# The output projection of two attentions in seven block products instead of eight

## The chip, the core and the metric

The kernel runs on one core of a Trainium2 chip, as one launch. The metric is the device time of that launch in microseconds. All data is float32. The engines are called by the profile's names: PE (TensorE matmuls), PEld (TensorE weight loads), DVE (VectorE), ACT (ScalarE), POOL (GpSimd) and SP (SyncE, which issues most of the DMAs).

## The reference

Four transformer layers run one after the other over x of shape (4, 256, 256) with a context of the same shape. The first layer, which the change touches, has two cross attentions and an MLP:

```python
B, D, H, K = 4, 256, 16, 128            # 4 batches of 256 tokens, 256 features, 16 heads of 128

def _cross_attention(q_in, kv_in, wq, bq, wk, bk, wv, bv, wo, bo, bias_k, bias_v):
    qh = (q_in @ wq + bq).reshape(b, q_len, H, K)      # wq, wk, wv: 256 x 2048
    kh = (kv_in @ wk + bk).reshape(b, t, H, K)
    vh = (kv_in @ wv + bv).reshape(b, t, H, K)
    kh = jnp.concatenate([kh, jnp.broadcast_to(bias_k, (b, 1, H, K))], axis=1)   # one learned key
    vh = jnp.concatenate([vh, jnp.broadcast_to(bias_v, (b, 1, H, K))], axis=1)   # and value
    logits = jnp.einsum('bqhk,bthk->bhqt', qh, kh) / sqrt(K)
    weights = jax.nn.softmax(logits, axis=-1)
    ctx = jnp.einsum('bhqt,bthk->bqhk', weights, vh).reshape(b, q_len, H * K)
    return ctx @ wo + bo                               # wo: 2048 x 256

x = x + _cross_attention(layer_norm(x), ctx, ...)      # first attention
x = x + _cross_attention(layer_norm(x), ctx, ...)      # second attention
x = x + gelu(layer_norm(x) @ w_fc1 + b_fc1) @ w_fc2 + b_fc2
...                                                    # three more layers, heads of 16 and 8 features
```

`ctx @ wo` is what the change computes in another way.

## The kernel before

**Tasks and a planner.** The kernel is written as a list of `Task` objects. A task has PE work (`run`, with a shape and an estimated length in us), the tasks it comes after, buffers that it takes from rings and gives back, and `Post` steps: work of another engine on what PE has left in PSUM, with estimated lengths in ns, such as an add on DVE. A Post may name two engines; the planner then takes the one that ends it first. `plan` goes through the tasks with a model of each engine's clock and writes down one order. Each engine then runs its own instructions strictly in that order (`Pinned` keeps them in program order). The table `HANDICAPS` steers the order: a number for each batch in each stage, one for each kind of task, and four general ones: `near` (a reserve, in us, that is added before a task counts as ready), `slack`, `solo` (a penalty for running one half of a pair of narrow products alone) and `wide` (a factor on the Posts' lengths). Nearly all instructions are issued through `Pinned`, so that the profile gives them all the same line, L134; tiles tell them apart.

**The first two attentions.** The loop over `li` runs over the two attentions, that over `hg` over four groups of four heads, and that over `bp` over two pairs of batches. For each group the weights are loaded into one of two sets of tiles (`W0`: `wv`, `wq`, `wk`, `wo` and others), by DMAs of SP. For each pair of batches V, q and k are each made by `seven`: two matrices are cut into 2 x 2 blocks, and the product of blocks is made in seven block products instead of eight, with sums of blocks made before on POOL (`sums`, `value_sums`) or on DVE or POOL (`differences`, `context_sums`), and sums of the products on DVE and ACT.

Then, for each batch and each half of its queries (128 rows), four heads are scored on PE (128 x 257, the learned key included), DVE takes the maximum of each row, ACT the exponential, and `quotients` on DVE multiplies each row by the reciprocal of its sum. The scores of one half lie in one tile `E` of the ring `E0`. For each head, the four 128 x 128 blocks of `E` of both halves are then transposed on PE (`turns`), copied to `eT`, and multiplied with V (`weighted`). The result of a head, 128 features x 256 tokens, is put into `cT` (ring `CT`) with its bias added.

**The projection.** When all four heads of a batch are in `cT`, `project` (task of 3.46 us) multiplies it with the group's `wo`: for each of two tiles of 128 tokens, four matmuls, one for each head, with 128 tokens as the stationary operand and 256 features as the moving one, all summed in PSUM. That fills one PSUM bank of 128 x 512. `add` on DVE then adds the bank to `X`, the residual, in one instruction. The projections come 2 x 4 x 4 = 32 times.

PSUM has eight banks, handed out by the ring `PS`. Of the buffers: `E0` has four tiles, `XN` (for the layer norm's output) three, `CT` two, and each of the two sets of weights has its own `bvl`, the row of learned values that is subtracted from the bias row `bvb`.

After the two attentions come the layer's MLP and the other three layers, planned in the same way, in stages 1 to 6 of the table.

Of the kernel before, what the change touches and what calls it, by code (L numbers as in the profile page):

```python
# [11 lines left out]
ALU = mybir.AluOpType  # L12
# [3 lines left out]
P = 128  # L16
B, S, D = 4, 256, 256
# [34 lines left out]
def kernel(ctx: ExitStack, tc: tile.TileContext, a: dict, out: bass.AP):  # L52
# [85 lines left out]
    def pe(out, lhsT, rhs, start, stop, **more):  # L138
        te.matmul(out, lhsT, rhs, start=start, stop=stop, **more)
# [69 lines left out]
    def Xb(b):  # L209
        return X[:, 2 * b : 2 * b + 2, :]  # L210
# [109 lines left out]
    class Layer:  # L320
# [629 lines left out]
    NG, HG = 4, 4  # L950
# [19 lines left out]
    def l0_ring(n, shape, tag):  # L970
        return Ring([l0.tile(shape, F32, tag=f"{tag}{i}", name=f"{tag}{i}") for i in range(n)])
# [4 lines left out]
                k: l0.tile(shape, F32, tag=f"{k}{i}", name=f"{k}{i}")  # L976
                for k, shape in (
                    ("wv", [P, 2, 512]), ("wq", [P, 2, 512]), ("wk", [P, 2, 512]), ("wo", [P, HG, D]),
                    ("bvb", [P, 512]), ("bvl", [P, 512]), ("t4", [P, 256]),
                )  # L980
            }
            for i in range(2)
# [241 lines left out]
    for li in range(2):  # L1224
# [35 lines left out]
        for hg in range(NG):  # L1260
            g = slice(hg * 512, (hg + 1) * 512)
            w = {}
            t_w = {}
            take = [(W0, w, "w")]
            for k in ("wk", "wv", "wq"):
                def run(e, k=k, li=li, g=g, w=w):
                    dma.dma_start(
                        w["w"][2][k], a[f"L0_xattn_{k}{li + 1}"][:, g].rearrange("(k p) n -> p k n", p=P)
                    )
# [7 lines left out]

            t_w["wo"] = load(0, [], "wo", run, 512, (), loads[-1:])

            def run(e, li=li, hg=hg, g=g, w=w):  # L1280
                dma.dma_start(w["w"][2]["bvb"], a["bv"][li : li + 1, g].to_broadcast([P, 512]))
                bv = _C0["bias_v"] + hg * HG
                dma.dma_start(
                    w["w"][2]["bvl"],
                    a[f"cols{li + 1}"][bv : bv + HG, :].rearrange("(o h) k -> o (h k)", o=1).to_broadcast([P, 512]),
                )

            t_bv = load(0, [], "bv", run, 512, (), [t_w["wv"]])

            def run(e, w=w):
                on = ve if e == "DVE" else ge
                on.tensor_tensor(w["w"][2]["bvb"], w["w"][2]["bvb"], w["w"][2]["bvl"], ALU.subtract)

            t_w["bv"] = Task(
                0, None, 0, None, [t_bv], posts=[Post(("DVE", "POOL"), {"DVE": 640, "POOL": 1300}, run, near=True)]
            )
            of_w = []
            for bp in range(2):  # L1300
                b0 = 2 * bp
# [12 lines left out]
                if li == 0 and hg == 0 and bp == 0:  # L1314
                    tV = []
                    for i in range(4):
                        v = {}

                        def products(i=i, u=u, v=v, w=w, bp=bp):
                            at_ = (4 * bp + i) * P  # L1320
                            for k in range(2):
                                pe(v["pt"][2], ctxT[:, k, at_ : at_ + P], w["w"][2]["wv"][:, k, :], k == 0, k == 1)

                        def add(e, i=i, u=u, v=v, w=w):
                            ve.tensor_tensor(u["V"][2][:, i, :], v["pt"][2], w["w"][2]["bvb"], ALU.add)
# [9 lines left out]
                else:  # L1335
# [3 lines left out]
                    def A(p, i, k, b0=b0):  # L1339
                        return ctxT[:, k, (b0 + p) * S + i * P : (b0 + p) * S + (i + 1) * P]  # L1340
# [72 lines left out]
                for bb in range(2):  # L1413
# [91 lines left out]
                    v = {}  # L1505
# [161 lines left out]
    def plan(handicap):  # L1667
# [82 lines left out]
        while open_:  # L1750
# [39 lines left out]

    HANDICAPS = (
        [
            [200, -1154, 94, -638],
            [-3409, 1715, -2929, -1548],
            [-4433, -221, 307, 3761],
            [-196, 3749, -2255, 1548],
            [-587, -3349, -2110, -1727],
            [3962, 4331, 1810, 3420],
            [-768, 201, 383, 800],
        ],  # L1800
        {
            (0, "<lambda>"): -32, (0, "columns.run"): 2, (0, "columns.scaled"): 14, (0, "context_sums.run"): -4,
            (0, "exp"): -195, (0, "fetch.run"): -64, (0, "learned"): -19, (0, "norm.apply"): 18,
            (0, "norm.stats"): 38, (0, "open_late"): 1, (0, "plus_row_to.run"): 5, (0, "products"): 296,
            (0, "project"): 12, (0, "quotients"): -4, (0, "rest_of.<lambda>"): -98, (0, "rows_of.<lambda>"): -14,
            (0, "run"): 3, (0, "scores"): 83, (0, "seven.first"): 268, (0, "seven.fourth"): 2,
            (0, "seven.third"): -24, (0, "sums.run"): -32, (0, "transposed.run"): 531, (0, "turns"): 2,
            (0, "value_sums.run"): -13, (0, "weighted"): 942, (1, "mlp.up"): 59, (1, "norm.apply"): -14,
            (1, "norm.root"): -17, (1, "norm.stats"): -68, (1, "run"): 65, (2, "attention.fetch"): -6,
            (2, "attention.hidden"): -81, (2, "attention.project"): -8, (2, "ending.turns"): -3, (2, "keys.run"): 15,  # L1810
            (2, "norm.apply"): 37, (2, "norm.root"): -59, (2, "norm.stats"): -147, (2, "plus_row_to.run"): 3,
            (2, "transposed.run"): 42, (2, "unit16.turns"): -169, (2, "unit16.weights"): 144,
            (2, "values.fill"): -21, (2, "values.run"): -263, (3, "mlp.down"): 842, (3, "norm.apply"): 51,
            (3, "norm.root"): 3, (3, "norm.stats"): -63, (4, "attention.fetch"): -7, (4, "attention.hidden"): -2,
            (4, "attention.project"): 773, (4, "ending.back"): -19, (4, "ending.turns"): -203, (4, "keys.plus"): 42,
            (4, "keys.run"): 189, (4, "plus_row_to.run"): 2, (4, "queries.run"): -76, (4, "transposed.run"): -76,
            (4, "unit16.maxima"): -36, (4, "unit16.turns"): 10, (4, "unit16.weights"): -527, (4, "values.fill"): 99,
            (4, "values.run"): 7, (5, "mlp.down"): 63, (5, "mlp.up"): 39, (5, "norm.root"): -215,
            (5, "norm.stats"): 10, (5, "plus_row_to.run"): -37, (5, "transposed.run"): 192,
            (6, "attention.<lambda>"): -15, (6, "attention.fetch"): -9, (6, "closing.apply"): -11,  # L1820
            (6, "closing.root"): -76, (6, "closing.stats"): -56, (6, "ending.back"): -133, (6, "keys.run"): -37,
            (6, "plus_row_to.run"): -51, (6, "queries.run"): -486, (6, "unit8.exps"): -89, (6, "unit8.scores"): -113,
            (6, "unit8.weighted"): 134, (6, "values.fill"): -1, (6, "values.run"): -126,
        },
        (0.4, 0.24, 0.71, 1.08),
    )
    for group, taken, behind in plan(HANDICAPS)[1]:
        for r, h, k, i in taken:
# [68 lines left out]
```

## Time and profile before

| | |
|---|---|
| Runs | 1351.6 us median of 3 (1349.92 to 1353.52) |
| The profiled execution | 1349.59 us |
| Its span, first to last instruction | 1347.8 us, granted TensorE clock 0.993 |
| Busy in the span | PE 1313.6 us, PEld 1050.7, DVE 813.5, ACT 691.3, POOL 218.4 |
| The first two attentions | up to about 710 us of the span; the last projection runs from 707.1 to 710.7 |
| Matmul records that read `wo` | 512 |

A float32 matmul shows as two records of PE, each with a record of its weight load on PEld; a transpose shows as one. The length of a matmul's record holds its way through the array; the distance from one record's start to the next is what it takes from PE. Rows of the windows give the stretch, its length, the busy time of PE, PEld, DVE, ACT and POOL in it (with the number of instructions), the granted clock, the DMA engines' share and GB/s. Rows of groups give line, engine, operation, out<-in, shapes and count, then busy us and mean ns of one, then the idle time of the engine just before them and what ended it. Rows of waits give who waited for whom: us in total, times, and the longest.

### The profile page before, as it was taken

Reading aid. Unit: us, or ns where it says so; the run is one execution under the profiler, and the core shown is the slowest. Engines: PE = TensorE matmul, PEld = TensorE weight load, DVE = VectorE, ACT = ScalarE, POOL = GpSimd, SP = SyncE. Lnnn points to the kernel's source line nnn. Section 1 sums busy time; section 2 is a strip of 40 time slices with the busy share of each in tenths; the row PEclk is TensorE's granted clock in tenths of the full one; section 3 lists DMA queues with packets and bytes.
Section 4 is the critical chain, followed back from the end, with each engine's and each line's share of the span. In section 5 each row is a group of like instructions: output and inputs, shape, how many; then the busy total and the mean of one; then the engine's idle time right before and its main releaser. Section 6 shows DMA issues by size and latency. Waiting matters only on the chain.

```text
span 1347.8 us, 22397 instructions
## 1 busy us (share of the span) xinstructions
PE 1313.6 (97%) x8523; PEld 1050.7 (78%) x8523; DVE 813.5 (60%) x2171; ACT 691.3 (51%) x1659; POOL 218.4 (16%) x385
## 2 busy tenths in 40 slices
PE   7999999999999999999999999999999999999897
PEld 4888888888888888888888877677667667767665
DVE  7765655766576746555443574665572565677686
ACT  3454444444345434445352244444545477868796
POOL 9420010200142002000015231030010020110000
PEclk9999999999999999999999998999999999999999
DMA  7010100202002001000024110000000000000000
GB/s 234 31 33 17 63 1 16 63 1 78 1 17 63 1 32 47 17 32 1 1 68 146 34 49 5 1 9 1 1 1 5 2 2 1 1 17 9 9 2 17
DMA packets 25627, 38.00 MB, mean 28 GB/s; under 512 B 2244, under 2 KB 16086, under 8 KB 25392
## 3 DMA queue, kind: packets, MB, share of 16 engines
q1 hardware_dynamic: 24640, 35.56, 8.1%
q0 software_dynamic: 608, 0.76, 0.4%
q8 instruction: 67, 1.10, 0.3%
q14 instruction: 40, 0.33, 0.1%
q10 hardware_dynamic: 272, 0.26, 0.1%
HBM read 35.52 MB, written 1.05 MB: 27 GB/s over the span
## 4 chain that ended last, share of the span: by engine, by line
PE 90%; DVE 7%; ACT 2%; issue 1%; DMA 1%; POOL 0%; SPq 0%; DVEq 0%; ACTq 0%
PE ps_o L134 23%; PE ps_pj L134 23%; PE ps_s L134 23%; PE ps_et L134 21%; DVE E L134 2%; DVE eq L134 1%; ACT eq L134 1%; DVE shift L134 1%; DMA wk<-in_L_xattn_wk_dram 1%; ACT qk L134 0%; DVE qk L134 0%; DVE X L134 0%; DVE e L134 0%; DVE craw L134 0%; DVE xo L134 0%
## 5 line engine op out<-in xcount | busy, mean ns | idle before, releaser
L134 ACT ACTIVATE eq<-eq,nm 128x256 f32<-128x256 f32 x256 | 106.1, 506 | 0.2 <-DVE nm L134 0.2
L134 DVE TENSOR_SCALAR E<-E,rinv 128x257 f32<-128x257 f32 x256 | 97.9, 445 | 2.3
L134 PE MATMUL ps_s<-qk 32*128 32x256 f32 (+1 forms) x270 | 85.2, 476 | 0.0
L134 POOL TENSOR_SCALAR mv<-mv 128x2 f32<-128x2 f32 (+1 forms) x32 | 7.4, 233 | 454.9 <-DVE mv L134 454.4
L134 PE MATMUL ps_o<-qk 32*128 32x256 f32 (+1 forms) x280 | 80.4, 458 | 0.0
L134 PE MATMUL ps_et<-qk 32*128 32x256 f32 (+1 forms) x232 | 75.3, 468 | 0.5 <-DVE V L134 0.5
L134 PE MATMUL ps_pj<-qk 32*128 32x256 f32 (+1 forms) x242 | 75.2, 470 | 0.0
L134 POOL COPY kT<-lks 128x4 f32<-128x4 f32 x32 | 5.8, 202 | 352.2 <-PE ps_et L134 122.5
L134 PE MATMUL ps_pj<-eq,qk 32*128 32x256 f32 x224 | 55.2, 405 | 0.0
L134 PE MATMUL ps_s<-eq,qk 32*128 32x256 f32 x212 | 50.7, 406 | 0.4 <-ACT qk L134 0.4
L134 DVE TENSOR_REDUCE shift<-ps_s 128x1 f32<-128x512 f32 (+1 forms) x54 | 36.5, 683 | 20.9 <-PE ps_o L134 11.3
L134 POOL TENSOR_TENSOR X<-X,rowbc 128x256 f32<-128x256 f32 x56 | 41.6, 764 | 40.9 <-DVE e L134 12.4
L134 PEld LDWEIGHTS ps_o<-qk 32*128 32x128 f32 x280 | 38.6, 188 | 7.8 <-issue 3.7
L134 PE MATMUL ps_o<-eq,qk 32*128 32x256 f32 x168 | 44.3, 401 | 0.3 <-ACT e L134 0.3
L134 PE MATMUL ps_et<-eq,qk 32*128 32x256 f32 x164 | 44.3, 413 | 0.0
L134 PEld LDWEIGHTS ps_s<-qk 32*128 32x128 f32 x270 | 37.7, 189 | 8.4 <-issue 4.9
L134 POOL TENSOR_SCALAR plus<-hide_r,rowof,bkx 128x256 f32<-128x256 f32 x32 | 17.7, 559 | 146.6 <-DVE qk L134 146.2
L134 DVE TENSOR_TENSOR X<-ps_o,X 128x256 f32<-128x256 f32 (+1 forms) x20 | 10.4, 518 | 51.2 <-PE ps_o L134 51.2
L134 DVE TENSOR_TENSOR X<-ps_pj,X 128x512 f32<-128x512 f32 (+1 forms) x18 | 10.3, 573 | 50.1 <-PE ps_pj L134 50.1
L134 DVE TENSOR_REDUCE shift<-ps_o 128x1 f32<-128x512 f32 (+1 forms) x47 | 31.8, 683 | 13.6 <-PE ps_et L134 5.4
L134 PEld LDWEIGHTS ps_et<-qk 32*128 32x128 f32 x232 | 33.4, 183 | 8.3 <-issue 3.5
L134 ACT ACTIVATE E<-ps_pj,nm 128x257 f32<-128x257 f32 x58 | 27.7, 481 | 22.2 <-DVE nm L134 22.2
(578 smaller groups left out, 3941.5 us busy)
## 6 DMA issues: line engine op xcount, KB each, us to landing
wk<-in_L_xattn_wk_dram SPq DMA_DIRECT2D x8, 512.0 KB, 3.8
wv<-in_L_xattn_wv_dram SPq DMA_DIRECT2D x8, 512.0 KB, 4.1
wq<-in_L_xattn_wq_dram SPq DMA_DIRECT2D x8, 512.0 KB, 5.5
wo<-in_L_xattn_wo_dram SPq DMA_DIRECT2D x8, 512.0 KB, 3.8
bvb<-in_bv_dram SPq DMA_DIRECT2D x8, 256.0 KB, 5.7
bvl<-in_cols_dram SPq DMA_DIRECT2D x8, 256.0 KB, 5.8
f<-in_L_xattn_w_fc_dram SPq DMA_DIRECT2D x2, 1024.0 KB, 5.1
f<-in_L_xattn_mlp_w_dram SPq DMA_DIRECT2D x2, 1024.0 KB, 5.4
```

The costliest lines, as they stand in the source:

```text
L134: return lambda *args, **more: tc.keep_in_program_order(f(*args, **more))
```

## The change

The projection of a batch and a head group, 256 tokens x 512 inner features times 512 x 256, is taken as two sums over pairs of heads, `p`. In each, the 256 x 256 matrix of `cT` is cut by token tile `i` and head `k`, and that of `wo` by head `k` and half of the 256 features `j`. The product of the 2 x 2 blocks is made in seven products of 128 x 128 blocks. The sums of blocks of `wo` are made on POOL once for each group (`wo_sums`, four instructions over both pairs of heads; one of them overwrites a block of `wo`), those of `cT` once for each batch and group on DVE or POOL (`tile_sums`, four instructions; one overwrites a block of `cT`). The products are not summed apart: they accumulate in three areas of 128 columns of one PSUM bank, and in between DVE adds an area to the blocks of `X` that need it so far. So the projection is four tasks, one after the other, with six adds of 128 x 128.

To make room, `E0` goes from four tiles to three, `XN` from three to two, and `bvl` becomes a ring of one; new are `SC` (two tiles for the sums of `cT`) and `TW` (one tile for those of `wo`). All numbers of `HANDICAPS` are replaced, for the later stages too.

```diff
-                    ("bvb", [P, 512]), ("bvl", [P, 512]), ("t4", [P, 256]),
+                    ("bvb", [P, 512]), ("t4", [P, 256]),
...
+    BVL = l0_ring(1, [P, 512], "bvl")
...
-    E0, ET, CT = l0_ring(4, [P, HG, S + 1], "E"), l0_ring(3, [P, 2, S], "eT"), l0_ring(2, [P, HG, S], "cT")
-    XN, UU = l0_ring(3, [P, 2, D], "xn"), l0_ring(3, [P, 512], "u")
+    E0, ET, CT = l0_ring(3, [P, HG, S + 1], "E"), l0_ring(3, [P, 2, S], "eT"), l0_ring(2, [P, HG, S], "cT")
+    XN, UU = l0_ring(2, [P, 2, D], "xn"), l0_ring(3, [P, 512], "u")
+    SC, TW = l0_ring(2, [P, 3, 2, P], "sc"), l0_ring(1, [P, 3, 2, P], "tw")
...
+            def wo_sums(e, w=w, tw=tw):
+                B_ = w["w"][2]["wo"].rearrange("p (q k) (j c) -> p q k j c", k=2, j=2)
+                B11, B12, B21, B22 = B_[:, :, 0, 0], B_[:, :, 0, 1], B_[:, :, 1, 0], B_[:, :, 1, 1]
+                T2, T3, T4 = (tw["t"][2][:, n] for n in range(3))
+                ge.tensor_tensor(T3, B22, B12, ALU.subtract)
+                ge.tensor_tensor(B12, B12, B11, ALU.subtract)
+                ge.tensor_tensor(T2, B22, B12, ALU.subtract)
+                ge.tensor_tensor(T4, B21, T2, ALU.subtract)
+
+            t_tw = Task(0, None, 0, None, [t_w["wo"]], takes=[(TW, tw, "t")], posts=[Post(("POOL",), 3250, wo_sums)])
...
-                    def project(c=c, v=v, w=w):
-                        for qt in range(2):
-                            for h in range(HG):
-                                pe(
-                                    v["pt"][2][:, qt * D : (qt + 1) * D], c["c"][2][:, h, qt * P : (qt + 1) * P],
-                                    w["w"][2]["wo"][:, h, :], h == 0, h == HG - 1,
-                                )
-
-                    def add(e, b=b, v=v):
-                        ve.tensor_tensor(Xb(b), v["pt"][2].rearrange("p (i d) -> p i d", i=2), Xb(b), ALU.add)
-
+                    def A(p, i, k, c=c):
+                        return c["c"][2][:, 2 * p + k, i * P : (i + 1) * P]
+
+                    def W(p, k, j, w=w):
+                        return w["w"][2]["wo"][:, 2 * p + k, j * P : (j + 1) * P]
+
+                    def tile_sums(e, c=c, sc=sc):
+                        on = ve if e == "DVE" else ge
+                        A = c["c"][2].rearrange("p (q k) (i t) -> p q k i t", k=2, i=2)
+                        A11, A12, A21, A22 = A[:, :, 0, 0], A[:, :, 1, 0], A[:, :, 0, 1], A[:, :, 1, 1]
+                        S2, S3, S4 = (sc["s"][2][:, n] for n in range(3))
+                        on.tensor_tensor(S3, A11, A21, ALU.subtract)
+                        on.tensor_tensor(A21, A21, A22, ALU.add)
+                        on.tensor_tensor(S2, A21, A11, ALU.subtract)
+                        on.tensor_tensor(S4, A12, S2, ALU.subtract)
+
+                    t_sc = Task(
+                        b, None, 0, None, tC, takes=[(SC, sc, "s")],
+                        posts=[Post(("DVE", "POOL"), {"DVE": 1400, "POOL": 3100}, tile_sums, near=True)],
+                    )
+
+                    def products(*which, A=A, W=W, v=v, sc=sc, tw=tw):
+                        def run():
+                            for at_, lhsT, rhs, start in which:
+                                for p in range(2):
+                                    pe(
+                                        v["pt"][2][:, at_ * P : (at_ + 1) * P],
+                                        A(p, *lhsT) if isinstance(lhsT, tuple) else sc["s"][2][:, lhsT, p, :],
+                                        W(p, *rhs) if isinstance(rhs, tuple) else tw["t"][2][:, rhs, p, :],
+                                        start and p == 0, True, skip_group_check=True,
+                                    )
+
+                        return run
+
+                    def add(i, j, at_, b=b, v=v, gives=()):
+                        def run(e):
+                            to = Xb(b)[:, i, j * P : (j + 1) * P]
+                            ve.tensor_tensor(to, v["pt"][2][:, at_ * P : (at_ + 1) * P], to, ALU.add)
+
+                        return Post(("DVE",), 215, run, gives=gives)
+
+                    t1 = Task(
+                        b, "full", 0.88, products((0, (0, 0), (0, 0), True), (1, (0, 1), (1, 0), False)),
+                        tC + [t_w["wo"], t_plus[b]], takes=[(PS, v, "pt")], posts=[add(0, 0, 0), add(0, 0, 1)],
+                    )
+                    t2 = Task(b, "full", 0.44, products((0, 0, 0, False)), [t1, t_sc, t_tw], posts=[add(1, 0, 0)])
+
+                    t3 = Task(
+                        b, "full", 0.88, products((0, (1, 0), (0, 1), False), (2, 1, 1, False)), [t2],
+                        posts=[add(1, 1, 0), add(1, 1, 2)],
+                    )
                     t = Task(
-                        b, "full", 3.46, project, tC + [t_w["wo"], t_plus[b]], takes=[(PS, v, "pt")],
-                        posts=[Post(("DVE",), 605, add, gives=[(PS, v, "pt")])], gives=[(CT, c, "c")],
-                    )
-                    finals[b].append(t)
+                        b, "full", 0.88, products((0, 2, (1, 1), False), (2, (1, 1), 2, False)), [t3],
+                        posts=[add(0, 1, 0), add(1, 0, 2, gives=[(PS, v, "pt")])], gives=[(CT, c, "c"), (SC, sc, "s")],
+                    )
+                    finals[b] += [t1, t2, t3, t]
...
-            freed_w.append(Task(0, None, 0, None, behind=of_w, gives=[(W0, w, "w")]))
+            freed_w.append(Task(0, None, 0, None, behind=of_w, gives=[(W0, w, "w"), (TW, tw, "t")]))
...
     HANDICAPS = (
...
-        (0.4, 0.24, 0.71, 1.08),
+        (0.08, 0.27, 25.35, 1.11),
```

The load of `bvl` and the subtraction from `bvb` take and give back the one tile of `BVL`; the lines for that are left out above, as are the two lists of `HANDICAPS`.

More of the change, by code (lines that the diff above doesn't have):

```diff
@@ L1278, with run @@
             t_w["wo"] = load(0, [], "wo", run, 512, (), loads[-1:])
-            def run(e, li=li, hg=hg, g=g, w=w):
+            vl = {}
+            def run(e, li=li, hg=hg, g=g, w=w, vl=vl):
                 dma.dma_start(w["w"][2]["bvb"], a["bv"][li : li + 1, g].to_broadcast([P, 512]))
@@ L1283, in run @@
                 dma.dma_start(
-                    w["w"][2]["bvl"],
+                    vl["l"][2],
                     a[f"cols{li + 1}"][bv : bv + HG, :].rearrange("(o h) k -> o (h k)", o=1).to_broadcast([P, 512]),
                 )
-            t_bv = load(0, [], "bv", run, 512, (), [t_w["wv"]])
-            def run(e, w=w):
+            t_bv = load(0, [], "bv", run, 512, [(BVL, vl, "l")], [t_w["wv"]])
+            def run(e, w=w, vl=vl):
                 on = ve if e == "DVE" else ge
-                on.tensor_tensor(w["w"][2]["bvb"], w["w"][2]["bvb"], w["w"][2]["bvl"], ALU.subtract)
+                on.tensor_tensor(w["w"][2]["bvb"], w["w"][2]["bvb"], vl["l"][2], ALU.subtract)
             t_w["bv"] = Task(
-                0, None, 0, None, [t_bv], posts=[Post(("DVE", "POOL"), {"DVE": 640, "POOL": 1300}, run, near=True)]
-            )
+                0, None, 0, None, [t_bv], posts=[Post(("DVE", "POOL"), {"DVE": 640, "POOL": 1300}, run, near=True)],
+                gives=[(BVL, vl, "l")],
+            )
+            tw = {}
+            def wo_sums(e, w=w, tw=tw):
[7 more added lines that the diff above has]
+            t_tw = Task(0, None, 0, None, [t_w["wo"]], takes=[(TW, tw, "t")], posts=[Post(("POOL",), 3250, wo_sums)])
             of_w = []
@@ L1504 @@
                     allC += tC
[L1505 to L1516 removed]
+                    v, sc = {}, {}
@@ L1792 @@
         [
[L1793 to L1799, printed above, removed]
-        ],
-        {
[L1802 to L1823, printed above, removed]
@@ new lines @@
+            [193, 234, 247, -3959],
+            [-2244, 3225, 2020, -3081],
+            [569, 1374, -1015, 5180],
+            [1576, 190, -1990, 1820],
+            [-965, -1653, -3726, -177],
+            [-606, 1461, -932, 475],
+            [-306, -5624, 918, -2557],
+        ],
+        {
+            (0, "columns.run"): 45, (0, "columns.scaled"): -10, (0, "context_sums.run"): -77,
+            (0, "differences.run"): -117, (0, "exp"): -1, (0, "fetch.run"): -4, (0, "norm.apply"): -228,
+            (0, "norm.root"): -72, (0, "norm.stats"): 307, (0, "open_late"): -1, (0, "plus_row_to.run"): 13,
+            (0, "products"): -21, (0, "products.run"): -65, (0, "quotients"): -207, (0, "rest_of.<lambda>"): -31,
+            (0, "rows_of.<lambda>"): 3, (0, "run"): 2, (0, "scores"): -22, (0, "seven.first"): -38,
+            (0, "seven.fourth"): -8, (0, "seven.second"): -36, (0, "seven.third"): -649, (0, "sums.run"): -2,
+            (0, "tile_sums"): 26, (0, "transposed.run"): 34, (0, "turns"): -751, (0, "weighted"): 490,
+            (1, "mlp.down"): -1017, (1, "mlp.up"): 24, (1, "norm.apply"): 24, (1, "norm.stats"): 38,
+            (1, "plus_row_to.run"): -8, (1, "run"): -1, (1, "transposed.run"): 18, (2, "attention.fetch"): -96,
+            (2, "attention.project"): -31, (2, "ending.back"): -5, (2, "ending.turns"): 1240, (2, "norm.root"): 4,
+            (2, "norm.stats"): 1, (2, "plus_row_to.run"): -57, (2, "queries.run"): 576, (2, "transposed.run"): -94,
+            (2, "unit16.maxima"): -1204, (2, "unit16.turns"): 518, (2, "unit16.weighted"): 451,
+            (2, "unit16.weights"): 29, (2, "values.fill"): -8, (2, "values.run"): 41, (3, "mlp.up"): 29,
+            (3, "norm.apply"): 80, (3, "norm.root"): 13, (3, "norm.stats"): -107, (3, "transposed.run"): -65,
+            (4, "attention.fetch"): 85, (4, "ending.back"): -16, (4, "ending.turns"): 244, (4, "keys.plus"): 7,
+            (4, "keys.run"): -21, (4, "plus_row_to.run"): -38, (4, "queries.run"): 102, (4, "transposed.run"): -80,
+            (4, "unit16.turns"): -2, (4, "unit16.weighted"): 387, (4, "unit16.weights"): -441, (4, "values.fill"): 3,
+            (4, "values.run"): -12, (5, "mlp.down"): 14, (5, "norm.apply"): 31, (5, "norm.stats"): -1,
+            (5, "plus_row_to.run"): -11, (5, "transposed.run"): 10, (6, "attention.<lambda>"): -73,
+            (6, "attention.fetch"): -22, (6, "closing.root"): -16, (6, "closing.stats"): 53, (6, "ending.back"): 68,
+            (6, "ending.turns"): -97, (6, "plus_row_to.run"): -2, (6, "queries.run"): 5, (6, "transposed.run"): -12,
+            (6, "unit8.scores"): -920, (6, "unit8.turns"): -574, (6, "unit8.weighted"): 66, (6, "values.run"): -220,
```

## The prediction

> **What bounds the kernel now.** I read the page first, for the busy shares and the chain of waits, then the busy time by stages, then single operations.
>
> ```profile
> PE 1313.6 (97%) x8523; PEld 1050.7 (78%) x8523; DVE 813.5 (60%) x2171; ACT 691.3 (51%) x1659; POOL 218.4 (16%) x385
> ...
> PE 90%; DVE 7%; ACT 2%; issue 1%; DMA 1%; POOL 0%; SPq 0%; DVEq 0%; ACTq 0%
> ```
>
> TensorE is busy 97% of the span and holds 90% of the chain. The changed stage is the first two attentions, from about 20 to 710 us; the windows (window, length, then busy time of PE, PEld, DVE, ACT, POOL) show how tight it is.
>
> ```profile
> 60.00:690.00 630.00, 626.86 (x3132) 549.38 (x3132) 384.83 (x877) 291.43 (x826) 72.98 (x123) 1.00 0.10 30
> 690.00:720.00 30.00, 27.71 (x139) 24.21 (x137) 5.10 (x14) 10.16 (x21) 9.99 (x32) 1.00 0.27 91
> 720.00:1348.00 628.00, 606.26 (x5032) 437.87 (x5031) 378.53 (x1174) 364.48 (x745) 88.69 (x151) 0.99 0.04 12
> ```
>
> From 60 to 690 us PE idles 630 - 626.86 = 3.1 us, at granted clock 1.00. VectorE is busy 384.8 / 630 = 61%, GpSimd 12%. So a microsecond of matmul taken out here is one off the end, unless something slower than PE appears; the later stages (21.7 us idle) keep their work.
>
> **The matmuls removed.** The instructions that read `wo` with `cT`, and who waited for them:
>
> ```profile
> L134 PE MATMUL ps_pj<-wo,cT x160: 379/379/382, 55.5 to 710.3; 128*128 128x256 f32 x160
> L134 PE MATMUL ps_s<-wo,cT x128: 377/379/382, 134.6 to 668.8; 128*128 128x256 f32 x128
> L134 PE MATMUL ps_et<-wo,cT x112: 379/379/382, 84.9 to 687.0; 128*128 128x256 f32 x112
> L134 PE MATMUL ps_o<-wo,cT x112: 377/379/382, 174.9 to 584.0; 128*128 128x256 f32 x112
> ...
>   DVE X L134: 87.8, 31
> ```
>
> That is 512 records: 32 projections (2 attentions x 4 head groups x 4 batches) of 8 matmuls, each f32 matmul two records. Their 379 ns is latency; what each costs is the distance to the next, from the timeline (start, length, count):
>
> ```profile
> 55.06 0.60 PE L134 MATMUL ps_s<-ident,E 128*128 128x128 f32 x4
> 55.50 3.62 PE L134 MATMUL ps_pj<-wo,cT 128*128 128x256 f32 x16
> ...
> 1090.23 1.10 PE L134 MATMUL ps_et<-w3v,ctxT 128*128 128x64 f32 x8
> ```
>
> A projection's 16 records: (3.62 - 0.379) / 15 = 0.216 us each, so 512 x 0.216 = 110.6 us in all. They stand in one run, with no wait inside it.
>
> **The matmuls added.** Seven products for each of two pairs of heads are 14 matmuls, 28 records, 896 in all, each with a moving operand of 128 columns instead of 256. No row is an f32 product of that shape. Below: half of 0.216 is 0.108, and the transposes, 128 columns with a load of their own each, come every (0.60 - 0.273) / 3 = 0.109 us. Above: the value products of the last attention, only 64 columns wide, come every (1.10 - 0.275) / 7 = 0.118 us; this is not half of the 128-column distance, so there the load of the weights sets it. I take 0.110, nearest to the transposes, because streaming 128 columns is just about as long as that load: 896 x 0.110 = 98.6 us. The gain is 12.0 us; at 0.109 it is 12.9, at 0.118 it is 4.9.
>
> One page speaks against this. The Trainium skill, "TensorE: Matmul & The Clock Gate", section "Back-to-back issue gap", gives 81 ns for each pair of weight load and 128-column matmul where the matmul alone takes 56 ns. If that ratio held here, as an estimate, 0.109 would become 0.158 us and the change would cost some 31 us instead of saving. The transposes above are such pairs and keep 0.109 us, so the sum does not use it.
>
> **VectorE and GpSimd work added.** The rows:
>
> ```profile
> L134 DVE TENSOR_TENSOR X<-ps_pj,X 128x512 f32<-128x512 f32 x10 | 6.9, 692 | 33.9 <-PE ps_pj L134 33.9
> L134 DVE TENSOR_TENSOR xo<-ps_et,rs 128x128 f32<-128x128 f32 x12 | 3.5, 291 | 0.4
> L134 DVE TENSOR_SCALAR E<-E,rinv 128x257 f32<-128x257 f32 x256 | 97.9, 445 | 2.3
> L134 POOL TENSOR_TENSOR f<-wq 128x256 f32<-128x256 f32 x16 | 11.9, 745 | 1.1 <-DMA wq<-in_L_xattn_wq_dram 0.4
> ```
>
> One add of 128x512 (0.692 us) becomes six of 128x128 (0.291, the nearest row from PSUM): 1.746 - 0.692 = +1.05 us, x 32 = 33.7 us of VectorE. `tile_sums` is four subtractions of 128x256 in SBUF: on VectorE at least 4 x 0.418 (the fastest `craw<-HT` of the same shape) = 1.67 us, x 32 = 53.5 us; on GpSimd 4 x 0.745 = 2.98 us, x 32 = 95 us. The planner's guesses (1.4 and 3.1) send most to VectorE; I assume two thirds, 36 us, and one third, 32 us, to GpSimd. `wo_sums` is always on GpSimd: 8 x 2.98 = 23.8 us.
>
> GpSimd's work is not free for VectorE. In the timeline:
>
> ```profile
> 254.59 3.18 DVE L134 TENSOR_SCALAR E<-E,rinv 128x257 f32<-128x257 f32 x4
> ...
> 254.48 0.73 POOL L134 TENSOR_TENSOR f<-wq 128x256 f32<-128x256 f32 x1
> 255.29 0.73 POOL L134 TENSOR_TENSOR wq<-wq 128x256 f32<-128x256 f32 x1
> ...
> 205.97 1.14 DVE L134 TENSOR_SCALAR E<-E,rinv 128x257 f32<-128x257 f32 x4
> ```
>
> Four quotients take 1.14 us alone and 3.18 us beside GpSimd's sums, each ending with one GpSimd instruction. By their median, 349 ns, the 256 quotients lose 256 x (0.445 - 0.349) = 24.6 us now to 73 us of GpSimd work, 0.34 us per us. The 56 us more there cost about 19 us of VectorE. In all VectorE gets 33.7 + 36 + 19 = 89 us: (385 + 83) / 619 = 76% of the stage, against 61%. That is cover, not bound, but its queue gets longer. What is late next is the softmax quotient in front of the transposes:
>
> ```profile
> PEld ps_et L134 <- DVE E L134: 2.3, 4, 1.1
> PEld ps_o L134 <- DVE E L134: 1.5, 2, 1.1
> PEld ps_pj L134 <- DVE E L134: 1.2, 3, 0.4
> ...
> PEld ps_s L134 <- DVE E L134: 0.5, 1, 0.5
> ```
>
> These waits are 5.5 us from 60 to 690. VectorE's free share falls from 39% to 24%; if waits grow inversely, 5.5 x 39 / 24 = 8.9, +3.4 us. Bounds: -3.1 (all present idling gone) and +25 (the first rival).
>
> **New waits.** Product t2 adds into columns that VectorE has just read, so it waits for both adds of t1, for `tile_sums` and for `wo_sums`; t3 and t4 wait for the adds before them. PE runs in order: the scores, transposes and seven-product blocks that the planner puts behind would stand too, but it counts a task as done after its adds and fills between. A handover costs at least two adds, 0.58 us. With other batches' work in between it is hidden; without, three are 1.7 us. That can happen where the second attention ends: there PE already waits 2.3 us (717.6 to 719.9) for the last batch's norm, so I add 1.7 once; bounds 0 and 1.7 for each of the two attentions.
>
> **Smaller buffers.** Three score buffers instead of four, two for the norm, one for the bias row, one for the `wo` sums. The bias row: its second DMA on SP now waits for the subtraction of the group before, with the next weights behind it; the queue has cover (DMA share 0.10), 0 us, and if not, one landing, 5.8 us, per group. The single `wo` sums tile: GpSimd can start only after the last projection of the group before; behind it stand the `kT` copies and the next weights' sums. The first projection of a group comes some 20 us after its first products, against 2.98 us of work: 0 us. Norm buffers: third norm waits for a first transpose, 0 to 1 us, nothing taken. The score buffers are the first rival.
>
> **Order numbers.** All planner numbers are new, also for the untouched later stages. They idle 21.7 us from 720 on; a third of that either way, 7 us, goes into the range, 0 into the sum. One of the numbers, the reserve after a predecessor, falls from 0.4 to 0.08 us, which leaves less for a late VectorE.
>
> **Sum.** The profiled execution took 1349.59 us (span 1347.8). 1349.6 - 12.0 + 3.4 + 1.7 = 1342.7. The median of the runs, 1351.6, is 2.0 above that execution, so the forecast is 1344.7 us, 0.5% less. About 0.3%, 4 us, can be told from no change: faster is under 1347.5, slower over 1355.7.
>
> **Rivals.**
>
> First, slower: three score buffers. In the timeline a batch's second half of scores (204.3 to 207.9) runs while the batch before still holds two buffers until its last transposes (from 218.6); all four are in use. With three, that half has to wait for those transposes, and its four quotients (4 x 0.349 + 0.167 for the reciprocal = 1.56 us) come just before PE wants them, with VectorE at 76%. There are 64 halves; if half are exposed, 32 x 1.56 = 50 us, and if PE has other work for half of each, 25 us. Then 1344.7 - 3.4 + 25 = 1366. It decides from 12 us of added waiting, 0.38 us a projection. For it: so little reserve and PE at 99.5% there. Against: the seven-product blocks (3 x 28 x 0.216 = 18 us of the 630 / 15 = 42 us per pair of batches) can be put into the gaps.
>
> Second, no change: the same mechanism at 0.2 to 0.4 us a projection, 6 to 13 us of waiting, which eats most of the 12: 1347.5 to 1355.7.
>
> Third, load and stream do not overlap at 128 columns: from the 64-column row, 0.118 plus 64 more columns (0.054) is 0.172 us, 896 x 0.172 = 154 us, 43 us slower: about 1393. The transposes speak against it.
>
> Fourth, the new order also removes a third of the later idling: 1338.
>
> **How the numbers follow.** The forecast, 1338 to 1347.5: 0.50. The larger gain: 0.07. No change: 0.17. Score buffers: 0.22. No overlap: 0.04. So faster 0.57, same 0.17, slower 0.26. The range leaves out the third rival, half of the first and the tip of the fourth: 1334 to 1364.
>
> **What would show it.** 896 records of 128 columns on `wo`, `sc` and `tw`, 0.109 to 0.112 us apart; PE busy 60 to 690 down by some 11 us for the same work; VectorE at 70 to 78% there; quotients' mean above 445 ns; waits of PE for `E` at 9 us or so. I am wrong if those waits pass 17 us, if the distance is over 0.123 us (then 896 records take what 512 did), or if the later stages move by more than 7 us.

## The result, and the profile after

The changed kernel takes 1344.42 us, the median of four runs (1343.91 to 1344.70); the kernel before takes 1351.79 (1349.92 to 1353.52) beside it. The ratio is 0.9949, 95% interval 0.9935 to 0.9963: 7.4 us faster, 0.3 us from the forecast. That nearness is mostly luck, as the experiments show: one term of the sum was too good, two sizeable ones were missing, and these two nearly cancel.

The page of the changed kernel, busy shares and then the chain of waits:

```profile
PE 1300.2 (97%) x8907; PEld 1041.9 (78%) x8907; DVE 869.0 (65%) x2473; ACT 696.3 (52%) x1670; POOL 246.7 (18%) x424
...
PE 89%; DVE 5%; ACT 3%; issue 1%; DMA 1%; SPq 1%; POOL 0%; DVEq 0%; ACTq 0%; POOLq 0%
```

PE is busy 13.4 us less (1313.6 - 1300.2), but the span is only 5.1 shorter (1347.8 - 1342.7): PE idles 42.5 us where it idled 34.2. The same windows as before, and then one over the end of the second attention, first of before, then of after:

```profile
60.00:690.00 630.00, 627.24 (x3537) 557.42 (x3536) 440.06 (x1173) 297.64 (x837) 100.72 (x159) 1.00 0.09 30
690.00:720.00 30.00, 26.54 (x147) 23.65 (x145) 7.96 (x28) 9.01 (x19) 6.44 (x25) 0.99 0.29 93
720.00:1343.00 623.00, 593.17 (x5000) 420.77 (x5000) 372.56 (x1163) 363.18 (x744) 90.65 (x153) 0.98 0.04 12
```
```profile
690.00:735.00 45.00, 42.71 (x211) 37.34 (x210) 11.32 (x33) 16.34 (x36) 21.24 (x54) 1.00 0.32 109
```
```profile
690.00:735.00 45.00, 31.23 (x161) 27.10 (x160) 12.64 (x39) 9.57 (x20) 15.40 (x45) 0.83 0.34 109
```

The attentions are as full as they were, with VectorE at 440 / 630 = 70%. Behind them is something new: 45 us in which PE works 31.2 instead of 42.7, and in which the granted clock falls to 0.83. The waits there (who waited for whom: us, times, longest), and the timelines of PE and GpSimd (start, length):

```profile
DVE e L134 <- POOL mv L134: 16.4, 1, 16.4
...
PE ps_et L134 <- DVE e L134: 12.1, 1, 12.1
POOL w3heads L134 <- DMA w3k<-in_L_xattn_Wk_dram: 8.4, 1, 8.4
```
```profile
714.65 1.89 PE L134 MATMUL ps_o<-HT,f 128*128 128x256 f32 x8
728.68 1.22 PE L134 MATMUL ps_et<-ident,e 128*128 128x128 f32 x4 [12.15 <-DVE e L134]
```
```profile
709.74 1.71 POOL L134 MEMSET shift<- 128x256 f32 x8 [21.76 <-PE ps_s L134]
...
716.04 1.10 POOL L134 TENSOR_SCALAR bqx<-cols,selq 128x2 f32<-128x2 f32 x4
725.59 1.47 POOL L134 COPY w3heads<-w3k 128x64 f32<-128x64 f32 x8 [8.45 <-DMA w3k<-in_L_xattn_Wk_dram]
727.14 0.22 POOL L134 TENSOR_SCALAR mv<-mv 128x2 f32<-128x2 f32 x1
```

PE pauses 12.15 us for the last norms of the layer (`e`). VectorE waits 16.4 us for their roots (`mv`), which stand in GpSimd's queue: the new order puts `w3heads`, eight copies that only the fourth layer reads, ahead of them, and these wait for a DMA that SP issues only at 719.6 us. Before, the roots ran at 718.3 and `w3heads` after them, at 726.6, and PE paused 2.3 us:

```profile
718.30 0.22 POOL L134 TENSOR_SCALAR mv<-mv 128x2 f32<-128x2 f32 x1
...
726.62 1.47 POOL L134 COPY w3heads<-w3k 128x64 f32<-128x64 f32 x8 [1.86 <-DMA w3k<-in_L_xattn_Wk_dram]
```
```profile
719.88 0.82 PE L134 MATMUL ps_et<-ident,e 128*128 128x128 f32 x4 [2.29 <-issue]
```

The projection itself. Its rows, one stretch in PE's timeline, and the new work on VectorE and GpSimd:

```profile
L134 PE MATMUL ps_o<-wo,cT x96: 270/275/378, 66.1 to 680.1; 128*128 128x128 f32 x96
```
```profile
65.62 0.60 PE L134 MATMUL ps_o<-kT,qT 128*128 128x257 f32 x2
66.06 1.05 PE L134 MATMUL ps_o<-wo,cT 128*128 128x128 f32 x8
66.95 0.60 PE L134 MATMUL ps_s<-kT,qT 128*128 128x257 f32 x2
...
70.42 0.61 PE L134 MATMUL ps_o<-tw,sc 128*128 128x128 f32 x4
```
```profile
L134 DVE TENSOR_SCALAR E<-E,rinv 128x257 f32<-128x257 f32 x256 | 80.7, 380 | 2.3
...
L134 DVE TENSOR_TENSOR sc<-cT 128x256 f32<-128x256 f32 x62 | 26.0, 419 | 1.1
...
L134 DVE TENSOR_TENSOR X<-ps_o,X 128x128 f32<-128x128 f32 x56 | 15.4, 287 | 5.2 <-PE ps_o L134 4.5
```

The eight records are (1.05 - 0.275) / 7 = 0.111 us apart; over all stretches 862 of the 896 distances have a median of 0.112, and the other 34 hold waits, 3.5 us in all. The projection is no longer one run: 114 stretches, with scores and transposes of other batches between. And PE's waits from 60 to 690 us have another cause than before (who waited for whom: us, times, longest):

```profile
PEld ps_o L134 <- DVE X L134: 2.8, 7, 0.7
PEld ps_s L134 <- DVE X L134: 2.3, 4, 0.7
PEld ps_pj L134 <- DVE X L134: 1.8, 7, 0.6
PEld ps_et L134 <- DVE X L134: 1.6, 6, 0.7
```

Before, these four lines named `E`, the quotients. Now they name `X`, the adds, and none of the waits of PE or PEld there is for `E`.

The span can be split by adding up, for each kind of PE record, the distance from its start to the next record's start, so that a wait is counted with the record before it:

| kind of record | before, us | after, us | difference |
|---|---|---|---|
| projection (`wo`, `sc`, `tw`) | 110.5 | 103.4 | -7.1 |
| scores of the attentions (128x257) | 111.0 | 113.8 | +2.8 |
| other products of 256 columns with a 128 x 128 stationary operand, the pause with them | 664.9 | 677.7 | +12.7 |
| narrow products of the later layers (32 rows) | 163.4 | 154.0 | -9.4 |
| all others | | | -5.1 |
| first record later | | | +0.95 |

That is -5.1 in the span. Three things are in it: the projection, the pause, and the later layers, which the change doesn't touch but whose order it replaces. A fourth cuts across the rows: the granted clock. Windows around its low stretches, first of before, then of after:

```profile
800.00:811.00 11.00, 10.32 (x76) 7.22 (x76) 10.93 (x24) 0.00 (x0) 0.95 (x2) 0.99 0.00 0
811.00:821.00 10.00, 10.00 (x58) 7.68 (x57) 8.09 (x16) 3.46 (x6) 4.28 (x6) 0.50 0.09 15
```
```profile
719.00:736.00 17.00, 5.69 (x16) 4.26 (x17) 4.78 (x12) 0.56 (x1) 9.73 (x21) 0.51 0.46 146
```

Up to PE's last matmul the clock was half for 10.2 us from 810.7 and 3.4 us from 1251.1 before, and for 17.1 us from 719.4, at the pause, after. If half of PE's time in these stretches, idling left out, is put down to the clock, it cost 6.8 us before and 3.1 us after, and 3.8 of the 6.8 us are in the narrow products. What brought it on at 810.7, where PE had been nearly full, isn't shown.

### The profile page after: what moved, and what is told of

Read it like the earlier page. It is cut to its first block, busy times and chain, and to the rows that moved or that the text cites. A ratio compares the mean times of both kernels' runs of the same rounds, so it can differ in the third digit from the quotient of the medians.

```text
span 1342.7 us, 23562 instructions
## 1 busy us (share of the span) xinstructions
PE 1300.2 (97%) x8907; PEld 1041.9 (78%) x8907; DVE 869.0 (65%) x2473; ACT 696.3 (52%) x1670; POOL 246.7 (18%) x424
## 3 DMA queue, kind: packets, MB, share of 16 engines
HBM read 35.52 MB, written 1.05 MB: 27 GB/s over the span
## 4 chain that ended last, share of the span: by engine, by line
PE 89%; DVE 5%; ACT 3%; issue 1%; DMA 1%; SPq 1%; POOL 0%; DVEq 0%; ACTq 0%; POOLq 0%
PE ps_s L134 23%; PE ps_o L134 23%; PE ps_et L134 22%; PE ps_pj L134 21%; ACT eq L134 1%; DVE nm L134 1%; DVE qk L134 1%; SPq L134 1%; DVE eq L134 1%; DVE shift L134 1%; DVE sc L134 1%; DVE X L134 1%; ACT e L134 0%; DMA w3k<-in_L_xattn_Wk_dram 0%; ACT qk L134 0%
## 5 line engine op out<-in xcount | busy, mean ns | idle before, releaser
L134 DVE TENSOR_SCALAR E<-E,rinv 128x257 f32<-128x257 f32 x256 | 80.7, 380 | 2.3
L134 PE MATMUL ps_o<-qk 32*128 32x256 f32 (+1 forms) x252 | 69.6, 478 | 0.4 <-DVE shift L134 0.4
L134 PE MATMUL ps_s<-qk 32*128 32x256 f32 (+1 forms) x264 | 69.4, 451 | 0.0
L134 DVE TENSOR_TENSOR X<-ps_s,X 128x128 f32<-128x128 f32 (+2 forms) x69 | 21.2, 316 | 37.8 <-PE ps_s L134 37.1
L134 DVE TENSOR_REDUCE nm<-ps_s 128x1 f32<-128x257 f32 x71 | 29.8, 420 | 19.2 <-ACT cT L134 10.3
L134 POOL TENSOR_TENSOR tw<-wo 128x256 f32<-128x256 f32 x16 | 11.7, 728 | 162.5 <-PE ps_et L134 83.3
L134 PE MATMUL ps_s<-kT,qT 128*128 128x257 f32 x142 | 41.4, 380 | 0.0
L134 PE MATMUL ps_o<-kT,qT 128*128 128x257 f32 x138 | 39.9, 380 | 0.0
L134 PEld LDWEIGHTS ps_pj<-qk 32*128 32x128 f32 x258 | 33.2, 184 | 6.4 <-issue 3.3
L134 ACT ACTIVATE E<-ps_s,nm 128x257 f32<-128x257 f32 x71 | 33.6, 474 | 8.2 <-DVE nm L134 8.2
```

The costliest lines, as they stand in the source:

```text
L134: return lambda *args, **more: tc.keep_in_program_order(f(*args, **more))
```

## The experiments

All kernels are made from the changed one. A control of it was timed again on the chip of e6 to e11; e1, e1b, e2, e4 and e12 ran on another. Each ratio is to the kernel of before on the same chip, whose medians differ by at most 0.5 us.

> The changed kernel again, as a control on the chip of the next three: 1344.4 us, 0.995 of before.

It took 1345.45 us (ratio to before 0.9954, 0.9937 to 0.9970).

**What the projection is worth: e2.** The order stays, with all four tasks in their places; in them run the eight old products of 256 columns, and one add of 128x512. The sums of blocks are left out.

```diff
-    for at_, lhsT, rhs, start in which:              # 14 products of 128 columns over four tasks
+    part = {((0, 0), (0, 0)): (0, 2), (0, 0): (2, 3), ((1, 0), (0, 1)): (3, 5), (2, (1, 1)): (5, 8)}
...
+    for n in range(lo, hi):                           # 2, 1, 2 and 3 of the 8 old products
```

> The changed kernel's plan and order, but the projection is the old one: eight matmuls of 256 columns, spread over the four tasks (2, 1, 2, 3), one add of 128x512 behind the last, and no sums on VectorE or GpSimd. The result is the reference's. Theory: 896 records at 0.112 us (100.4 us) become 512 at 0.216 (110.6), +10.2 us, and the waits of PE for the adds in between, 3.3 us, go: 1351 us. Rival: the load that the change puts on VectorE costs nothing and neither do the waits: +12 us, 1356 us. Second rival: the change's gain is all order, the projection itself is worth nothing: 1344 us.

1347.15 us (0.9967, 0.9954 to 0.9980), between its theory (1351) and its second rival (1344). So the seven products are worth 1.7 us against the control, 2.7 against the first median, of the 7.4. That is little, but the lowest of e2's runs, 1345.95, lies above the highest of the control, 1345.64. The rest comes from elsewhere, the order above all. In e2's trace the projection's records take 110.5 us again and the scores 2.7 less, and the waits for `X` are gone from the lists: the 10 us that the matmuls save come back mostly as waits for adds.

**Where the products' gain went: e7 and e6.** e7 leaves out all adds but the last two of each projection:

```diff
+    if (i, j, at_) not in ((0, 1, 0), (1, 0, 2)):
+        return
```

> The changed kernel without the four adds of 128x128 in the middle of each projection (behind its first three tasks); the last two stay. It leaves out part of the sum into X. Theory: PE waits some 3.3 us in all for those adds, because the next product adds into columns that VectorE still reads; without them 1341 us. VectorE has 128 x 0.287 = 37 us less. Rival (the prediction's step): what costs is VectorE's load, by the quotients in front of the transposes; then this gives back 37 of the 89 us of load, 1.4 us: 1343 us.

1337.91 us (0.9899, 0.9884 to 0.9913): 7.5 us under the control, twice what the theory gave these waits. (The code has seven adds a projection, not six, and five of them are left out here, not four: 64 records remain of 224.) e6 keeps the adds and leaves out the sums over `cT` and `wo`:

> The changed kernel without the sums of blocks (tile_sums on VectorE, wo_sums on GpSimd); the products read blocks of cT and wo in their place. It leaves out part of the computation. Theory: these 52 us of VectorE and 24 us of GpSimd are covered, PE does not wait for them: 1344 us, no change within 1 us. Rival (the prediction's step): the load makes the quotients late, 3.4 us: 1341 us.

1339.28 us (0.9907, 0.9892 to 0.9922): 6.2 us under the control. The theory that the sums are covered fell. The waits show how:

```profile
PEld ps_o L134 <- DVE X L134: 1.5, 5, 0.5
PEld ps_pj L134 <- DVE X L134: 1.3, 4, 0.6
...
PEld ps_et L134 <- DVE X L134: 0.4, 2, 0.2
...
PEld ps_s L134 <- DVE X L134: 0.2, 1, 0.2
```

PEld's waits for `X` fall from 8.5 to 3.4 us. One such place in the changed kernel:

```profile
112.98 0.42 DVE L134 TENSOR_TENSOR sc<-cT 128x256 f32<-128x256 f32 x1
...
114.42 0.42 DVE L134 TENSOR_TENSOR sc<-cT,sc 128x256 f32<-128x256 f32 x1
114.76 0.61 DVE L134 TENSOR_TENSOR X<-ps_s,X 128x128 f32<-128x128 f32 x2
...
115.43 0.52 PEld L134 LDWEIGHTS ps_s<-tw,sc 128*128 128x128 f32 x4 [0.67 <-DVE X L134]
```

VectorE works in order. The two adds that the second task waits for stand behind the four sums of the same projection, 4 x 0.42 = 1.7 us in one block, which that task needs as well. So VectorE does 2.3 us of work one after the other before PE can go on, and leaving out either part ends the wait: most of the two gains is one and the same. Of the 24 waits for `X` in PEld's lines, 12 (5.0 us) are of this kind; in 8 (1.9 us) the adds stand behind a block of quotients, and in 4 (1.6 us) behind neither. 31 of 32 blocks of sums are on VectorE.

**The pause: e1 and e1b.** e1 issues the eight copies `w3heads` later in GpSimd's queue, and nothing else; e1b does so with the filling of constants for two later layers as well (its additions are in the second condition).

```diff
-    for group, taken, behind in plan(HANDICAPS)[1]:
+    held_back = []
+    for n, (group, taken, behind) in enumerate(plan(HANDICAPS)[1]):
+        if group[0] is t_w3:                          # e1
+        if group[0] in (t_w3, t_L[2], t_L[3]):        # e1b
+            held_back.append(behind[0])
+            continue
...
+        if n == 1640:
+            for p, e, load in held_back:
+                p.run(e)
```

> The changed kernel, in which one GpSimd step alone, the copy of the last layer's key weights (w3heads), is issued 108 steps of the plan later; every other engine's order is the same. Theory: in the changed order this copy stands ahead of the norm of the last batch, waits for a DMA, and PE idles 12.3 us at 716 us, against 2.3 us before, with a lower granted clock behind it. Without it: 10 us of idling and some 2 us of clock are gone, 1344.4 - 12 = 1332 us. Rival: the idling is only moved, since the later layers wait for the same weights and for GpSimd anyway: 1342 to 1346 us.

> As e1_late_heads, and the two steps that make the constants of the third and fourth layer on GpSimd (3.6 us, ahead of the same norm) are issued late as well. Theory: the norm of the last batch then follows the constants of the second layer at once; the 2.3 us that were left at this place go too: 1330 us. Rival: PE has other matmuls until then, so no more than e1_late_heads: 1332 us.

1334.96 us (0.9873, 0.9858 to 0.9888) and 1328.77 us (0.9830, 0.9814 to 0.9846). A step of GpSimd in the wrong place of its queue cost 10.5 us against the control (9.5 against the first median), the two fillings another 6.2 us. The window over the end of the attention in e1b:

```profile
690.00:735.00 45.00, 43.98 (x231) 38.90 (x230) 14.94 (x45) 13.49 (x29) 14.72 (x32) 1.00 0.34 110
```

PE is busy 44.0 of 45 us, and the granted clock keeps 1.00. (In e1 PE still pauses 2.2 us, and the clock is half for 6.8 us.) The theory of the pause holds, and the sizes fit: from the changed kernel's profiled execution to that of e1b PE idles 12.6 us less, the half clock takes 3.1 us less, and the span is 15.6 us shorter.

**Does the projection pay without the pause: e9.** e1b with e2's old products in it.

> The changed kernel with the late fills and late head columns of e1b, and in it the old eight products of 256 columns spread over the four tasks, one add of 128x512, and no sums (as in e2). The question is whether seven products still pay once the pause behind the second attention is gone. Theory (pause and projection are independent, and the seven products are worth the 1.7 to 2.7 us that e2 showed): 1330.5 to 1331.5, slower than e1b's 1328.8. Rival (the pause hid work of VectorE, so that the sums and adds cost more once it is gone): 1328 or less.

1331.15 us (0.9853, 0.9835 to 0.9870), 2.4 above e1b. Within what the runs can tell, the products are worth the same with and without the pause.

**Sums on GpSimd: e10.** e1b, and in `tile_sums`:

```diff
-    on = ve if e == "DVE" else ge
+    on = ge
```

> e1b with the sums over cT (tile_sums) all on GpSimd, in the same places of the order; 31 of 32 were on VectorE. Theory (the adds that PE waits for stand behind these sums on VectorE, worth some 5 us by e6, and GpSimd has room): 40 us leave VectorE, 31 x 2.98 = 92 us go to GpSimd, which slow VectorE by the 0.34 us per us that the trace of before showed, 31 us, so that about a quarter of the 5 us is left: 1326 to 1328. Rival (the second task of the projection now waits for the slower sums, 2.98 us instead of 1.27, each time): 31 x 1.7 = 53 us at most, half of it covered: 1350.

1325.83 us (0.9814, 0.9796 to 0.9831), the fastest of all: 1.4% under the changed kernel. Its waits, and groups of VectorE and GpSimd, from 60 to 690 us:

```profile
PEld ps_o L134 <- DVE X L134: 1.0, 2, 0.8
...
PEld ps_pj L134 <- DVE X L134: 0.8, 2, 0.6
...
PEld ps_et L134 <- DVE X L134: 0.2, 1, 0.2
```
```profile
L134 DVE TENSOR_SCALAR E<-E,rinv 128x257 f32<-128x257 f32 x240 | 85.5, 420 | 2.1
...
L134 POOL TENSOR_TENSOR sc<-cT 128x256 f32<-128x256 f32 x64 | 47.3, 739 | 352.4 <-ACT cT L134 336.6 <-DVE cT L134 9.3 <-DVE E L134 4.0
```

The waits for `X` fall to 2.0 us, and no wait for the sums takes their place, although each now takes 0.74 instead of 0.42 us. The quotients pay: 85.5 us where e1b has 72.4, that is 13.1 us for 90.3 us more of GpSimd (191.0 against 100.7): 57 of the 240 quotients now run beside GpSimd work, at 0.64 us on the mean, where it was 10 in e1b; alone they take 0.35 us in both. With the sums there, the seven products are worth 1331.15 - 1325.83 = 5.3 us.

**The order numbers: e11 and e12.** e11 plans the changed kernel with the table of before; e12 sets back one number, `solo`.

```diff
-        (0.08, 0.27, 25.35, 1.11),
+        (0.08, 0.27, 0.71, 1.11),                     # e12
```

> The changed kernel with the order numbers of before, so that its structure (seven products, smaller buffers) is planned by numbers that were found for another structure. Theory (of the 7.4 us, 2.7 are the products and the rest the order, which is a pause of about +10 behind the attentions and about -9 to -14 in the later stages): no pause, later stages as before, thus 1351.8 - 2.7 = 1349, give or take 5 for what the planner does with new tasks in the attentions. Rival (the numbers fit only the structure they were found for, and PE waits in the attentions as well): over 1356.

> The changed kernel with one order number set back: the penalty for one half of a pair of narrow products (32 rows) alone, from 25.35 to 0.71. The order up to the second layer stays as it is, attentions and pause included; in the later layers it has 38 halves alone and 109 pairs, where it had 128 pairs and none alone (before: 16 alone, 120 pairs). Theory (the later layers of the changed kernel gain because all narrow products run in pairs): by the traces of before and after, 8 pairs taken apart cost 163.4 - 154.0 = 9.4 us of 32-row records, 1.2 us each, so 19 pairs cost 22 us: narrow products at 176 us, the run at 1367. Rival (the pairs are not it, the rest of the new numbers is): narrow products within 4 us of 154, the run at 1344 to 1350.

e11 took 1419.98 us (1.0501, 1.0462 to 1.0539). The theory missed by 71 us, and its rival has the direction: with the old numbers PE stands idle 17.4 us behind records of the projection (0.4 in the changed kernel), 14.5 of them in one pause behind the last, and the last that read `wo` come 40 us later (748.6 instead of 708.9 us). The larger part is in the later layers: they hold 48 halves alone, the narrow products take 206.0 us instead of 154.0, and the granted clock from 720 us to 1343 is 0.95 (0.98 in the changed kernel). A table of this kind belongs to the program that it was found for. e12 took 1391.50 us (1.0298, 1.0274 to 1.0322), 47 us more than the changed kernel for one number. Up to 735 us the two agree:

```profile
60.00:690.00 630.00, 627.24 (x3537) 556.80 (x3536) 439.93 (x1172) 297.67 (x837) 100.72 (x159) 1.00 0.09 30
690.00:735.00 45.00, 31.46 (x162) 27.30 (x161) 12.74 (x39) 9.57 (x20) 15.42 (x45) 0.82 0.34 109
```

Behind, the narrow products take 188.2 us instead of 154.0. Of these 34.2 us, 6.0 are more idling of PE behind them and 5.6 are stretches at half clock. The other 22.6 us for 19 pairs taken apart are 1.2 us each, as the theory had it. The direction is settled, and with it most of the -9.4 us in the table above, which divide in the same way into -7.7 us of products, -3.8 of clock and +2.1 of idling: before had 16 halves alone, the changed kernel has none. The other 13 us of e12 come with the new order of the later layers and weren't followed further.

**Two that tell less.** e4 was a first try at the pairs: every eighth pair is issued lane after lane instead of in turns.

```diff
+            pairs += 1
+            if pairs % 8 == 0:
+                for lane in lanes:
+                    for _ in lane:
+                        pass
+                lanes = []
```

> The changed kernel, in which 16 of the 128 pairs of narrow matmuls (32 rows each, in the last three layers) are issued one half after the other instead of interleaved; nothing else is changed. The kernel before issued 16 halves alone, that is 8 pairs less. Theory: a pair costs as much as one half, 1.1 to 1.2 us, so 16 splits add 16 x 1.17 = 19 us: 1363 us, and the eight pairs that the new order numbers made were worth some 9 us. Rival: the halves lie beside waits of the softmax, so that splitting them costs little: 1344 to 1350 us.

1344.58 us (0.9946, 0.9931 to 0.9961): no effect, and the narrow products take 154.1 us, as before the edit. Of the 16 pairs 6 have only one turn a half, so the order of issue changes in 10. There the trace shows the two halves starting together as before, so this took no pair apart and says nothing on what a pair is worth; e12 does. e8 halves the stationary operand, to ask what sets 0.112 us.

```diff
-    v["pt"][2][:, at_ * P : (at_ + 1) * P],
+    v["pt"][2][:64, at_ * P : (at_ + 1) * P],         # and 64 columns of lhsT, 64 rows in the adds
```

> The changed kernel, in which each of the projection's products loads only 64 of the 128 token columns as weights, and the adds take 64 partitions. It leaves out half of the projection. Theory: the 0.112 us between the new records are set by the weight load, not by the 128 columns that stream; with half the load they come every 0.109 us as the transposes do, 896 x 0.003 = 2.7 us less in all: 1341.7 us. Rival: the distance is that of the stream and stays 0.112.

1374.34 us in a single run: some 30 us slower, with half the weights to load. The timeline at the place shown above:

```profile
66.54 0.60 PE L134 MATMUL ps_o<-kT,qT 128*128 128x257 f32 x2
67.07 1.09 PE L134 MATMUL ps_o<-wo,cT 128*64 128x128 f32 x8
68.09 0.70 PE L134 MATMUL ps_s<-kT,qT 128*128 128x257 f32 x2
```

From the score before it to the projection it is 0.53 us (0.44 in the changed kernel), through the eight records to the next score 1.02 (0.89). Over all 114 stretches the record ahead of a stretch, its first, its last and the record behind it take 31 us more than in the changed kernel, 0.28 us a stretch: it is the edges that cost, and they make up the whole loss, 29.9 us in the span. Inside the stretch the median distance is 0.109, as the theory had it, and not the rival's 0.112. But rows written and adds were halved together with the load, so what sets 0.112 is left open, and the edges hide what 0.003 us would bring.

## Why the prediction was right, and where it was not

The sum was -12.0 + 3.4 + 1.7 + 0 = -6.9 us in the profiled execution; measured are -5.1 in the span and -7.4 in the medians. Point by point:

- **Matmuls, -12.0: mis-sized by a little.** The distance is 0.112, not 0.110: 896 x 0.112 = 100.4, so -10.2 us. The choice of the transposes as the nearest row was right, and the third rival (0.172) fell. The Trainium skill's ratio ("TensorE: Matmul & The Clock Gate", section "Back-to-back issue gap"), which would have made it 0.158 as an estimate, is not what these f32 products show: 0.112.
- **Waits for quotients, +3.4: wrong in kind, and too small.** PE's waits come from the adds. e7 and e6 show 6 to 7.5 us. The prediction named the new waits (t2 to t4 wait for the adds before them) and priced them at nothing where other batches' work lies between. The step that failed is that sentence: what lies between on PE is not enough when the add stands behind 1.7 us of sums on VectorE. The quotients' mean was to rise above 445 ns; it fell to 380. 31 of 32 sums went to VectorE, not two thirds, and in the new order 21 of the 256 quotients ran beside GpSimd work (0.70 us on the mean) where 66 had (0.72); alone they took 0.35 us in both. VectorE's share was to be 76% and is 70%. The seven adds were counted as six; with 7 x 0.287 they are 42.1 us more on VectorE, not 33.7.
- **So the projection, -12.0 + 3.4 = -8.6, is -1.7 to -2.7** (e2; e9: 2.4). The waits have the size of the "no change" rival, 6 to 13 us, but not its mechanism, which was the score buffers.
- **End of the attentions, +1.7: wrong cause, wrong size.** A pause was expected there, from handovers. It is 12.15 us instead of 2.3, from a copy for the fourth layer in GpSimd's queue; e1 and e1b take 15.7 to 16.7 us off by moving such steps, some 3 of them by the granted clock. Nothing in the profile of before shows it, but the diff does: with all order numbers new, each step of GpSimd at that seam could move.
- **Order of the later layers, 0 with 7 us either way: wrong, and by the prediction's own sign.** The narrow products gave 9.4 us. The bound came from PE's idle time there, but two halves alone keep PE busy for longer than a pair: the gain was in busy time, 7.7 us of products and 3.8 of clock, with 2.1 us more of idling. The diff showed the number (0.71 to 25.35), and e12 shows what it moves. This is the fourth rival's direction by another mechanism. The granted clock has no term in the sum; over the whole span it took 3.7 us less than before.
- **Smaller buffers: right as far as the waits show.** No run of the changed kernel has the old buffers, but no wait for `E` is among PE's waits from 60 to 690 us, and the first rival fell.

So the forecast was right in sign and size because errors cancelled. Between the two profiled executions, the -5.1 us are -2.6 of products (e2's span against the changed kernel's), +9.9 of idling at the pause, -7.7 of pairs, -3.7 of clock, and another -1.0 that is left open. The forecast had -8.6 for the first and +1.7 for all the others together. The medians differ by 2.2 us more than these two executions: the profiled one of before, 1349.59, is faster than the four runs of its median.

## What to carry to other kernels

When a product is cut into blocks that accumulate through adds in between, price the queue of the engine that adds: the longest block of work that can stand ahead of an add, times the number of times that PE waits for one. Moving that block to an idle engine gave 2.9 us here (e1b to e10), more than the seven products gave with the sums on VectorE (2.4). When a change brings a new order, treat the order as a second change: list what was moved on each queue at the seams between stages, and bound it by busy time too, not by idle time alone. And put an engine's early work for late stages behind what the next stage waits for: moving such steps gave 15.7 to 16.7 us here, over twice the change's gain.

## What the hardware showed that was not expected

A switch between stationary operands of 128 and of 64 columns cost time on both sides of it (e8, medians over 114 stretches): going in, the record before takes 0.09 us longer and the first one 0.05; coming out, the last one takes 0.09 us longer and the record behind it 0.06 to 0.10. Two products of 32 rows overlap the same whether they are issued in turns or one after the other (e4, ten pairs: 154.1 us against 154.0). GpSimd's block sums slowed VectorE's quotients by 13.1 us for 90.3 us of more work, 0.15 us per us (e10), where the trace of before gave 0.34; what counts is how many quotients run beside it. In the 45 us with the 12.15 us pause the granted clock was 0.83, and without the pause 1.00 (e1b). But it also fell to 0.50 for 10.2 us in the kernel of before, where PE had been busy 10.3 of the 11 us ahead.
